# A macaron block on one core: the third pass's matmuls split once more in groups of four tiles, and x added by accumulating transfers

## The chip, the core and the metric

The kernel runs on one core of a Trainium2 chip. The metric is device microseconds of one execution. A core has five engines, each with an instruction queue of its own: TensorE (PE, with weight loads shown apart as PEld), VectorE (DVE), ScalarE (ACT), GpSimd (POOL) and SyncE (SP). DMA transfers are issued from the queues of SP, ACT and POOL. An issue that has to wait holds up everything behind it in its queue.

## The reference

4 x 1024 tokens of 1024 channels go through a feed-forward layer, an attention layer and the same feed-forward layer again, in float32:

```python
dots = softmax(x @ centroids.T / 0.1)              # 64 clusters
hits = dots > 0.01
query_sel, cluster_sel = any(hits, axis=1), any(hits, axis=0)
dense = x @ weight.T + bias
ffn = where(query_sel[:, None] & cluster_sel[assignments][None, :], dense, 0)

x = x + 0.5 * ffn(layernorm(x))
x = x + attention(layernorm(x))
x = x + 0.5 * ffn(layernorm(x))
```

Which output columns of the feed-forward layer count (`cluster_sel`) is known only when all tokens have been through the gate. The attention mixes heads within one token.

## The kernel before, in words

**Tiles and passes.** The 4096 tokens are 32 tiles of 128 (`NT` = 32). A tile is one row buffer of 128 partitions x 1024 float32, 512 KB; all such buffers come from one pool of 26 (`row`, L147, `ROWS`). Pass 1 is the first feed-forward layer (dense product and gate), pass 2 the attention, with the gate and the last 256 columns of the second feed-forward layer (L1347 to the end of the loop), and pass 3 the other 768 columns of that layer, then the mask, the addition of x and the store of the output. Between passes tiles lie in device memory: `y2` holds x after the attention, `xTd` the normalised transposed tile, `d2` the dense product's last 256 columns. Of the tiles 26 to 31 (`KEPT` = 6) x, the transposed tile and the product stay in row buffers from pass 2 to pass 3; they are not stored to `y2`, `xTd`, `d2`.

**Seven block products.** The 768 columns are computed for two tiles at a time with Winograd's form of Strassen's algorithm (`winograd`, L315): tokens x channels and channels x columns are split 2 x 2, and seven block products instead of eight are made, each four matmuls of 128 x 128 by 384 columns (`HALF`). `token_sums` (L293) makes sums s1 to s4 of the tokens on POOL, and `weight_sums` made sums t1 to t4 of the weights in the space of `wqkv`. Results of several products add up in the same PSUM bank (`onto=`), and DVE adds each partial result to the tile's row (L328) and to the bias.

**The inner split of pass 1.** For tiles 4 to 27, pass 1 already works in groups of four tiles (`Group`, L649). Products 1, 5 and 6 are made whole, two tiles each (`outer`, L688). Products 2, 3, 4 and 7, of two tiles x 512 channels x 384 columns, are split once more in the same way: seven inner products, each two matmuls by 192 columns (`inner_product`, L796). It needs sums of the tokens' quarters (`inner_sums`, L636: four POOL operations of 256 columns) and 16 quarter sums of the weights (`inner`). The order of work inside a group is written out by hand: `inner_product` runs its own matmuls and reads and calls `fills` (matmuls of another product) and `works` (DVE work of other tiles) at fixed places. Every engine's queue has exactly the order of the code.

**Pass 3** (L1484 to L1575). For each pair of tiles SP loads the transposed tile, x from `y2`, and the 256 columns from `d2` (`load_3`, L1493), two pairs ahead. POOL adds the bias to the 256 columns and makes the token sums of the next pair (`ahead_3`, L1501). PE runs the seven products. DVE reads the banks, multiplies the row by the row mask and column mask (`masked`, L456), adds x (L1513), and ACT issues the store (`stored`, L1508). The pair 30/31 comes first, because its inputs are in row buffers, then 0/1 to 24/25; the masks and adds of the kept tiles are spread over the first pairs. In the last pair, products 7 and 4 are made in halves of 192 columns, and `finish` (L1545) masks, adds and stores each half straight from the bank.

In pass 2 POOL has, among others, the key expansion (L1196), the attention's scaling and addition of x (L1283, L1287), the store of `y2` (L1359) and of `d2` and `xTd` (L1304, L1305), and at the end the weight sums for pass 3 (L290) and the token sums of the first pairs.

Of the kernel before, what the change touches and what calls it, by code (L numbers as in the profile page):

```python
# [15 lines left out]
P = 128  # L16
# [26 lines left out]
def kernel(  # L43
# [270 lines left out]

    def winograd(a, b, ss, ts, pool, name, held=False, finish=None):  # L315

# [10 lines left out]
        def add(out, ps, other):  # L327
            nc.vector.tensor_tensor(out, ps, other, ALU.add)  # L328
# [31 lines left out]
        yield  # L360
        if finish:
            m = HALF // 2
            ys = [(prod(f"7{i}", s3, t3[:, :, sl]), sl) for i, sl in enumerate((slice(m), slice(m, HALF)))]
            for y, sl in ys:
                add(cb[:, 1, sl], y, ca[:, 1, sl])
        else:
            y = prod(7, s3, t3)
            add(cb[:, 1], y, ca[:, 1])
        if held:
# [14 lines left out]
        yield  # L384
        if finish:
            for y, sl in ys:
                finish(prod(4, a22, t4[:, :, sl], onto=y), sl)
        else:
            prod(4, a22, t4, onto=y)
            add(cb[:, 0], y, cb[:, 0])  # L390
        del xT[a], xT[b]
# [84 lines left out]
    with (  # L476
# [144 lines left out]

        M = HALF // 2
        inner = wqkv.rearrange("p k c -> p (k c)").rearrange("p (s k c) -> p s k c", s=16, k=2)

# [3 lines left out]

        def inner_weights():

            for i, y in enumerate((w21, ts[3], ts[2], w22)):
                yield from weight_sums(
                    quarters(y), [inner[:, 4 * i + j] for j in range(4)], [nc.gpsimd] * 4
                )
# [14 lines left out]
        class Group:  # L649
# [6 lines left out]
            def upper_sums(self):  # L656
                a, b = self.t[:2]
                self.i[2] = inner_sums(xT[a][:, 4:], xT[b][:, 4:], f"2_{a}")

            def sums_0(self):  # L660
# [134 lines left out]

            def inner_product(self, n, fills, works):  # L796

# [12 lines left out]
                s = self.i.pop(n)  # L810
                r1 = 1 + o % 2
                dst = (a, b) if n in (2, 3) else (c, d)

                def mul(j, src, wt, onto=None):
                    ps = onto
                    if onto is None:
                        ps = psum1.tile([P, 512], F32, tag="st", bufs=4, name=f"in{n}{j}_{a}")[:, :M]
                    for k in range(2):
                        nc.tensor.matmul(  # L819
                            ps,  # L820
                            src[:, k, :],
                            wt[:, k, :],
                            start=(k == 0 and onto is None),
                            stop=(k == 1),
                            skip_group_check=onto is not None,
                        )
                    return ps
# [12 lines left out]
                read(0, 0, u)  # L840
                works[0]()
                v = mul(7, s[:, 2], u3)
                fills[0]()
                read(1, 1, v)
                mul(6, s[:, 1], u2, onto=u)
                read(1, 0, u)
                works[1]()
                fills[1]()
                mul(4, hi[:, 2:], u4, onto=v)
                read(1, 0, v)  # L850
                del v
                mul(5, s[:, 0], u1, onto=u)
                read(1, 1, u)
                z = mul(2, lo[:, 2:], y21)
                works[2]()
                read(0, 0, z)
                del z
                fills[2]()
                mul(3, s[:, 3], y22, onto=u)
                read(0, 1, u)  # L860
                works[3]()
# [240 lines left out]
    with (  # L1102
# [192 lines left out]
        def has(t):  # L1295
            return 0 <= t < NT
# [29 lines left out]
        for s in range(NT + 5):  # L1326
# [29 lines left out]
            if s == NT:  # L1356
                next(sums)
            if g >= 0 and g < FIRST_KEPT:
                nc.gpsimd.dma_start(out=y2[g], in_=xt[g])  # L1359
# [128 lines left out]

    with (
        tc.tile_pool(name="psum3", bufs=1, space=bass.MemoryType.PSUM) as psum3,  # L1490
    ):

        def load_3(t):  # L1493
            if t not in xT:
                load_xT(t)
            load_x(t, y2[t], 3)
            dt_[t] = row(f"d4_{t}")
            lo = PARTS[2][0]
            nc.sync.dma_start(out=dt_[t][:, lo:], in_=d2[t][:, lo:])

        def ahead_3(a):  # L1501

            for t in (a, a + 1):
                tail = dt_[t][:, PARTS[2][0] :]
                nc.gpsimd.tensor_tensor(tail, tail, brow[:, PARTS[2][0] : EMB], ALU.add)
            return token_sums(xT, a, a + 1, 2)

# [3 lines left out]
        def added(t, sl=slice(0, EMB), store=True):  # L1511
            masked(dt_[t], t, 1, mask, sl)
            nc.vector.tensor_tensor(xt[t][:, sl], xt[t][:, sl], dt_[t][:, sl], ALU.add)  # L1513
            if store:
                stored(t, sl)

        gates_used()
        for t in range(2):
            load_3(t)
        t = NT - 2  # L1520
# [6 lines left out]
        mask = row_mask(clusters, hot, 1)  # L1527
        ss = ahead_3(0)
        kept = iter(range(FIRST_KEPT, NT))
        next(steps)  # L1530
        added(next(kept))
        next(steps)
        added(next(kept))
        for _ in range(2):
            next(steps)
        for t in range(2, 4):
            load_3(t)
        done = iter(())
        for a in range(0, FIRST_KEPT, 2):
            last = a + 2 == FIRST_KEPT  # L1540
            for t in (a + 4, a + 5):
                if t < FIRST_KEPT:
                    load_3(t)

            def finish(ps, sl):  # L1545
                t = FIRST_KEPT - 1
                d = dt_[t][:, sl]
                nc.vector.scalar_tensor_tensor(
                    d, ps, qsel[1][:, t : t + 1], mask[:, sl], ALU.mult, ALU.mult
                )  # L1550
                nc.vector.tensor_tensor(xt[t][:, sl], xt[t][:, sl], d, ALU.add)
                stored(t, sl)

            steps = winograd(a, a + 1, ss, ts, psum3, 3, finish=finish if last else None)
            if not last:
                ss = ahead_3(a + 2)
            tail = slice(2 * HALF, EMB)
            part = slice(0, HALF), slice(HALF, 2 * HALF)
            for i in range(7):
                next(steps)  # L1560
                for t in done if i in (0, 1 if last else 2) else kept if i in (4, 5) else ():
                    added(t)
                    break
                if a + 4 == FIRST_KEPT and i in (4, 5):
                    added(a + i - 2, tail)
                if last:

                    for t, sl in {
                        2: ((a, part[0]),),
                        3: ((a + 1, part[0]),),  # L1570
                        4: ((a + 1, part[1]),),
                        5: ((a, part[1]),),
                    }.get(i, ()):
                        added(t, sl, store=i != 3)
            done = iter((a, a + 1))  # L1575

# [42 lines left out]
```

## Time and profile before

| | us |
|---|---|
| median of three runs | 1290.11 (1288.87 to 1292.22) |
| the profiled execution | 1289.28 |
| its span, from the first to the last instruction | 1287.5 |
| PE, DVE, ACT, POOL busy | 1270.3, 927.9, 469.0, 724.2 |
| granted TensorE clock | 1.00 |
| pass 3: first products of pair 30/31 at, last matmuls from | 1028.4, 1280.9 |

In a line of the profile, `out<-in` are the program's names of the tiles an instruction writes and reads, `xN` is a count, and the brackets at the end give idle time before it and what ended that. Matmuls overlap, so the duration of one is longer than the distance between two; the pace is read from the starts. A float32 matmul of the code shows as two MATMUL records.

### The profile page before, as it was taken

How to read it: one execution, taken by the hardware profiler on the slowest of the kernel's cores; microseconds unless marked ns; L12 is line 12 of the kernel's file. 1: busy time of each engine (PE TensorE's matmuls, PEld its weight loads, DVE VectorE, ACT ScalarE, POOL GpSimd, SP SyncE). 2: the span in 40 equal slices, each digit the busy share in tenths (PEclk: the TensorE clock that was granted, in tenths of full speed). 3: DMA queues.
4: the chain of work that ended last, by engine and by line, in shares of the span. 5: the costliest groups of instructions: out<-in, count | busy, mean ns of one | idle time of the engine just before them, and what ended most of it. 6: DMA issues, size and time to landing. Idle time of an engine off the chain costs nothing.

```text
span 1287.5 us, 23368 instructions
## 1 busy us (share of the span) xinstructions
PE 1270.3 (99%) x8970; PEld 872.5 (68%) x8970; DVE 927.9 (72%) x1862; ACT 469.0 (36%) x736; POOL 724.2 (56%) x624
## 2 busy tenths in 40 slices
PE   8999999999999999999999999999999999999998
PEld 7578898898885666666666666666665655555555
DVE  5657777777777368888888888888876348555546
ACT  4312222222301356766666676666632300000000
POOL 2981533533534457666787877776747416633440
PEclk9999999999999999999999999999999999999999
DMA  9553545554555357677677777777561257565422
GB/s 308 110 164 84 147 117 122 173 162 135 169 192 195 92 161 230 182 202 219 220 225 223 223 217 237 224 221 236 157 188 31 102 163 255 202 213 192 174 107 82
DMA packets 191127, 227.12 MB, mean 176 GB/s; under 512 B 118184, under 2 KB 146728, under 8 KB 191016
## 3 DMA queue, kind: packets, MB, share of 16 engines
q1 hardware_dynamic: 170892, 171.33, 45.0%
q0 software_dynamic: 11232, 37.49, 8.4%
q10 hardware_dynamic: 8892, 16.81, 3.7%
q8 instruction: 71, 1.16, 0.4%
q14 instruction: 40, 0.33, 0.1%
HBM read 134.59 MB, written 90.99 MB: 175 GB/s over the span
## 4 chain that ended last, share of the span: by engine, by line
PE 84%; DVE 8%; DMA 3%; ACT 2%; POOL 2%; issue 1%; SPq 0%; DVEq 0%; ACTq 0%; POOLq 0%
PE st L337 27%; PE qs L1140 14%; PE ff L263 10%; PE in L819 8%; PE la L736 7%; PE st L700 7%; PE pq L263 3%; PE tp L230 3%; PE po L1258 2%; PE sc L1216 2%; DVE d L458 1%; DMA qkvd<-qkv 1%; POOL wqkv L290 1%; DVE bn L170 1%; DVE o L1270 1%
## 5 line engine op out<-in xcount | busy, mean ns | idle before, releaser
L263 PE MATMUL ff<-wc,xT 128*128 128x320 f32 x640 | 179.3, 433 | 2.2 <-DVE d L328 1.2
L263 PEld LDWEIGHTS ff<-wc,xT 128*128 128x128 f32 x640 | 119.9, 190 | 51.5 <-ACT xT L231 1.5
L337 PE MATMUL st<-wqkv,ts 128*128 128x384 f32 (+1 forms) x392 | 129.6, 480 | 2.1 <-POOL wqkv L290 2.1
L328 DVE TENSOR_TENSOR d<-st,d 128x384 f32<-128x384 f32 (+1 forms) x102 | 55.9, 551 | 96.3 <-PE st L337 95.5
L500 ACT ACTIVATE xb<-xb,scb 128x256 f32<-128x256 f32 x108 | 56.0, 590 | 162.0 <-DVE d L837 67.9
L1140 PE MATMUL qs<-wc,ts_2q 128*128 128x384 f32 x336 | 114.4, 490 | 0.0
L337 PE MATMUL st<-wc,xT 128*128 128x384 f32 x320 | 110.0, 487 | 0.0
L337 PEld LDWEIGHTS st<-wqkv,ts 128*128 128x128 f32 x392 | 73.9, 190 | 52.5 <-POOL wqkv L290 2.3
L469 POOL TENSOR_TENSOR x<-x,d 128x1024 f32<-128x1024 f32 x32 | 75.4, 2358 | 55.0 <-DVE d L458 40.1
L302 POOL TENSOR_TENSOR ts<-xT 128x512 f32<-128x512 f32 x20 | 25.7, 1285 | 140.9 <-PE st L337 74.7
L1196 POOL TENSOR_TENSOR kd<-qk,tmask 128x1024 f32<-128x1024 f32 x32 | 60.6, 1894 | 77.4 <-DMA qk<-qkvd 77.4
L458 DVE SCALAR_TENSOR_TENSOR d<-d,qsel,mask 128x1024 f32<-128x1024 f32 (+2 forms) x68 | 95.0, 1397 | 0.2
L1140 PEld LDWEIGHTS qs<-wc,ts_2q 128*128 128x128 f32 x336 | 62.6, 190 | 43.7 <-issue 3.2
L337 PEld LDWEIGHTS st<-wc,xT 128*128 128x128 f32 x320 | 60.4, 190 | 41.5 <-issue 0.6
L1287 POOL TENSOR_TENSOR x<-x,ot 128x1024 f32<-128x1024 f32 x32 | 78.2, 2445 | 2.5
L1140 PE MATMUL qs<-wqkv,xT 128*128 128x384 f32 x224 | 78.3, 492 | 0.0
L231 ACT COPY xT<-tp 128x512 f32<-128x512 f32 x112 | 59.4, 581 | 46.9 <-PE tp L230 46.9
L665 POOL TENSOR_TENSOR os<-xT 128x512 f32<-128x512 f32 x12 | 15.2, 1270 | 101.0 <-DVE sc L179 101.0
L837 DVE TENSOR_TENSOR d<-in,d 128x192 f32<-128x192 f32 (+1 forms) x168 | 64.9, 398 | 9.0 <-PE in L819 5.1
L700 PE MATMUL st<-ws,os 128*128 128x384 f32 x192 | 65.8, 486 | 0.0
L230 PEld LDWEIGHTS tp<-ident,xn 128*128 128x128 f32 x448 | 56.9, 191 | 12.9 <-issue 2.0
L220 ACT ACTIVATE xn<-x,sc 128x1024 f32<-128x1024 f32 x30 | 49.9, 1664 | 37.3 <-DVE sc L215 37.3
(197 smaller groups left out, 2764.4 us busy)
## 6 DMA issues: line engine op xcount, KB each, us to landing
x<-in_L_attn_x_dram SPq DMA_DIRECT2D x64, 512.0 KB
d<-d SPq DMA_DIRECT2D x64, 512.0 KB
out_dram<-x ACTq DMA_DIRECT2D x30, 512.0 KB
xb<-in_L_attn_x_dram SPq DMA_DIRECT2D x108, 128.0 KB
y<-x POOLq DMA_DIRECT2D x26, 512.0 KB, 3.8
xTd<-xT POOLq DMA_DIRECT2D x26, 512.0 KB, 6.0
xT<-xTd SPq DMA_DIRECT2D x26, 512.0 KB
x<-y SPq DMA_DIRECT2D x26, 512.0 KB
```

Source lines behind the costliest of these rows:

```text
L230: nc.tensor.transpose(tp[:, j, :], channels(xn)[:, k], ident)
L263: nc.tensor.matmul(p, src[:, k, :], wts[:, k, lo:hi], start=(k == 0), stop=(k == KT - 1))
L337: nc.tensor.matmul(ps, src[:, k, :], wts[:, k, :], start=(k == 0 and onto is None), stop=(k == 3), skip_group_check=onto is not None,)
L458: nc.vector.scalar_tensor_tensor(d[:, sl], d[:, sl], qsel[which][:, t : t + 1], mask[:, sl], ALU.mult, ALU.mult)
L469: nc.gpsimd.tensor_tensor(xt[t], xt[t], dt_.pop(t), ALU.add)
L700: nc.tensor.matmul(ps, src[:, k, :], wt[:, k, :], start=(k == 0 and n == 1), stop=(k == 3), skip_group_check=n != 1,)
L736: nc.tensor.matmul(ps[:, i], src[:, k, :], wt[:, k, :], start=(k == 0 and i == 0 and first is not None), stop=(k == 3), skip_group_check=i ...
L819: nc.tensor.matmul(ps, src[:, k, :], wt[:, k, :], start=(k == 0 and onto is None), stop=(k == 1), skip_group_check=onto is not None,)
L837: nc.vector.tensor_tensor(v, ps, v, ALU.add)
L1140: nc.tensor.matmul(ps, src[:, k, :], wts[:, k, :], start=(k == 0 and onto is None), stop=(k == 3), skip_group_check=onto is not None,)
L1196: nc.gpsimd.tensor_tensor(kd, qk[:, :, D:].unsqueeze(2).to_broadcast([P, NBLK, 4, D]), tmask.unsqueeze(1).unsqueeze(3).to_broadcast([P, NB ...
L1287: nc.gpsimd.tensor_tensor(xv, xv, ov, ALU.add)
```

## The change

Pass 3 takes pass 1's scheme for tiles 0 to 23, in six groups of four; the pair 24/25 goes ahead of them and stays as it was.

- Inner products: `inner_product` is turned into a generator, `parts`, and pass 3 runs two of them side by side (`both`): products 2 and 4, then 7 and 3. Between the inner products stand the outer ones (5 of this group, 1 and 6 of the next) and DVE's work: masks of the group before, s1 and s2 of the next group (512 columns each, DVE in place of POOL), the bias of the 256 columns (DVE in place of POOL).
- The 16 quarter sums of the weights are made again, by DVE, in a tile of their own.
- x is no longer loaded for these tiles. After the mask, a transfer from POOL's queue reads `y2` and adds it to the row in place (`accum_op=ALU.add`), and the store follows it. This also holds for the pair 24/25 and the kept tiles, whose x is now stored to `y2` in pass 2 (six more stores). Tiles 20 and 21 of the last group load x and add it on DVE and, for one part, on POOL.
- The last pair's halves and `finish` go; in the last group products 2 and 3 are interleaved by hand, and the last inner product is masked and added straight from the bank.

```diff
-    def winograd(a, b, ss, ts, pool, name, held=False, finish=None):
+    def winograd(a, b, ss, ts, pool, name, held=False):
...
-            if g >= 0 and g < FIRST_KEPT:
+            if has(g):
                 nc.gpsimd.dma_start(out=y2[g], in_=xt[g])
...
+            def sums_12(self, engine, which=(0, 1)):
...
+                for i in which:
+                    lo, hi = self.t[i], self.t[i + 2]
+                    engine.tensor_tensor(s1[:, i], xT[hi][:, :4], xT[hi][:, 4:], ALU.add)
+                    engine.tensor_tensor(s2[:, i], s1[:, i], xT[lo][:, :4], ALU.subtract)
...
+        def summed(t):
+            xt[t] = dt_[t]
+            nc.gpsimd.dma_start(out=xt[t], in_=y2[t], accum_op=ALU.add)
+            stored(t, slice(0, EMB))
+
+        def finished(t):
+            masked(dt_[t], t, 1, mask)
+            summed(t)
...
+        def both(x, y, fills, works):
+            for p in (x, y):
+                next(p)
+            works[0]()
+            fills[0]()
+            for p in (x, y, x, y):
+                next(p)
+            works[1]()
+            fills[1]()
+            for p in (x, y):
+                next(p)
+            works[2]()
+            for p in (x, y, x, y):
+                next(p)
+            works[3]()
+            for p in (x, y):
+                next(p)
+            fills[2]()
+            for p in (x, y):
+                next(p)
+            works[4]()
...
+            if not last:
+                g.sums_34()
+                for t in nxt.t:
+                    load_tail(t)
+                both(
+                    g.parts(2, w_bank),
+                    g.parts(4, w_bank),
+                    (lambda: g.outer(5, 0), lambda: g.outer(5, 1), lambda: nxt.outer(1, 0)),
+                    (
+                        one_masked(0),
+                        one_masked(1),
+                        then(one_masked(2), summing(0, 1)),
+                        one_masked(3),
+                        then(summing(2, 3), lambda: nxt.sums_12(nc.vector, (0,))),
+                    ),
                 )
...
+                nxt.lower_sums()
...
+                    nxt.upper_sums()
+                    nxt.sums_3(False)
+                both(
+                    g.parts(7, w_bank),
+                    g.parts(3, w_bank),
+                    (lambda: nxt.outer(1, 1), lambda: nxt.outer(6, 0), lambda: nxt.outer(6, 1)),
+                    (
+                        lambda: nxt.sums_12(nc.vector, (1,)),
+                        lambda: tail_biased(nxt.t[2]),
+                        lambda: tail_biased(nxt.t[3]),
+                        then(lambda: tail_biased(nxt.t[0]), lambda: early_tail(0)),
+                        then(lambda: tail_biased(nxt.t[1]), lambda: early_tail(1)),
+                    ),
+                )
+            else:
+                a, b, c, d = g.t
+                g.outer(5, 0)
+                g.outer(5, 1)
+                g.upper_sums()
+                g.sums_4()
+                both(
+                    g.parts(7, w_bank),
+                    g.parts(4, w_bank),
+                    (nothing,) * 3,
+                    (
+                        one_masked(0),
+                        one_masked(1),
+                        then(one_masked(2), summing(0, 1)),
+                        one_masked(3),
+                        summing(2, 3),
+                    ),
+                )
...
+                x, y = g.parts(2, w_bank), g.parts(3, w_bank)
+                first, second = slice(0, HALF), slice(HALF, 2 * HALF)
+                next(x)
+                next(x)
+                masked(dt_[d], d, 1, mask)
+                summed(d)
+                next(y)
+                next(x)
+                masked(dt_[c], c, 1, mask)
+                summed(c)
...
+                added(b, second)
+                next(y)
+                added(a, second, store=False)
+                y.send(last_part)
```

A generator of `parts` makes, in order: inner product 1; 7; 6 (onto the bank of 1); 4 (onto the bank of 7); 5 (onto the bank of 1); 2 (a bank of the other pool); the read of 2; 3 (onto the bank of 1). `one_masked(j)` masks a tile of the group before, or in the first group finishes the pair and makes quarter sums; `summing` issues the accumulating transfers and the stores; `sums_34` makes s3 and s4 and the inner sums of products 7 and 3 on POOL, `lower_sums` and `upper_sums` those of products 4 and 2.

## The prediction

> **What bounds the kernel now.** I read the engine table first, then the chain of waits, then the order of time on TensorE (PE).
>
> ```profile
> PE 1270.3 (99%) x8970; PEld 872.5 (68%) x8970; DVE 927.9 (72%) x1862; ACT 469.0 (36%) x736; POOL 724.2 (56%) x624
> ```
>
> PE is busy 99% of the span. The chain, asked from 950 us on, ends so:
>
> ```profile
> 1038.35 245.35 PE st L337 x776
> 1283.70 0.03 issue
> 1283.72 0.43 DVE d L1548
> 1284.15 0.02 issue
> 1284.17 0.36 DVE x L1551
> ```
>
> From 1038 us the third pass is one unbroken run of matmuls, then 0.8 us of VectorE (DVE), and 1287.50 - 1284.53 = 2.97 us of store and end. So PE time saved there is span saved, unless another engine or a transfer becomes late. How fast small matmuls go is read in the first pass, where groups of four tiles already use the inner split. PE in order of time (start, duration of the merged row; the next row's start tells the pace):
>
> ```profile
> 102.37 0.81 PE L819 MATMUL in<-wqkv,is 128*128 128x192 f32 x4
> 103.02 0.81 PE L819 MATMUL in<-ws,xT 128*128 128x192 f32 x4
> 103.67 2.74 PE L700 MATMUL st<-ws,os 128*128 128x384 f32 x8
> 106.25 0.81 PE L819 MATMUL in<-ws,is 128*128 128x192 f32 x4
> ```
>
> Four records of 192 columns take 0.65 us (102.37 to 103.02), eight of 384 take 2.58 us (103.67 to 106.25). (The code's two matmuls show as four records, its four as eight.) Half the columns thus cost 0.504 of the time: the split loses almost nothing here. The row means in the groups' view (326 and 486 ns) would say 0.67 and turn the change into a loss; they are latencies of overlapping matmuls and must not be used.
>
> The Trainium skill, page "TensorE: Matmul & The Clock Gate", section "Back-to-back issue gap", speaks against small matmuls: with weight loads between, a sustained stream is paced by both, and it gives 81 ns at 128 columns where streaming alone would be 56 ns. If 192 columns cost 45% over their share, a four-record chunk would take some 0.94 us (an estimate from that page) and the change would lose about 5 us a group; the rows above show that this does not happen at this shape.
>
> **The change, part by part.**
>
> *Matmuls.* Per four tiles the old code runs two pairs of seven products, 14 x 2.58 = 36.12 us (the steps at 1061.60, 1064.18, 1066.76 us are 2.58 apart throughout). The new code keeps products 1, 5, 6 (two tiles each, 6 x 2.58 = 15.48) and makes the other four by seven inner products of 0.65 each: 4 x 7 x 0.65 = 18.20. Together 33.68, so 2.44 us less; six groups: **-14.6 us**. Tiles 24 and 25 stay a pair and only move ahead.
>
> *Six more y2 stores on POOL.* A POOL store of y takes 0.60 us (its 26 issues: 15.5 us) and waits about 0.30 us for the add before it (7.7 us over 26). Late in the second pass POOL is once on PE's path:
>
> ```profile
> 954.31 1.89 POOL L1196 TENSOR_TENSOR kd<-qk,tmask 128x1024 f32<-128x1024 f32 x1 [16.37 <-DMA qk<-qkvd]
> ```
> ```profile
> 978.65 2.85 PE L337 MATMUL st<-wqkv,ts 128*128 128x384 f32 x8 [2.12 <-POOL wqkv L290]
> ```
>
> Stores of tiles 26 and 27 vanish in the 16.4 us of idle; that of 28 falls after it and before the weight sum that PE awaits; those of 29 to 31 come behind it. **+0.9 us**.
>
> *DVE inside the groups.* A group needs 21 reads of 192 columns, 7 of 384, 8 outer reads, four masks, four sums s1/s2 of 512 columns, and four tail biases. Rows: 0.348, 0.548, 0.555, 1.385 (third pass, 1050 to 1230 us), 0.425 for 256 columns; 512 lie between 0.557 (384) and 1.545 (1024), about 0.72. Sum 7.3 + 3.8 + 4.4 + 5.5 + 2.9 + 1.7 = 25.7 us beside 33.7 of PE. It is uneven: the half with products 2 and 4 holds all masks, about 15.5 us in 16.84; the other half holds 10. Laid out chunk by chunk, the tightest chain in the full half is the fifth inner product's result, read at 13.7 us, against PE's third product onto the same bank at 15.5: 1.9 us of slack. So 0. The old adds of x (1.5 us a tile) are what makes room.
>
> *Inner weight sums, and the start.* Sixteen DVE subtractions of 384 columns, 16 x 0.557 = 8.9 us. Eight lie beside pair 24/25 (DVE there: 5.0 of reads, 5.5 of masks, 4.5, 1.7 of biases, in 18.06 us), eight in group 0, where only two masks are due. Each set is finished at least 3 us before its product. POOL's sums for group 0 (16 of 256 columns at 0.73, 8 of 512 at 1.27, 22 us) have from about 1045 to 1094 us. 0.
>
> *Accumulating transfers.* No row shows one. PE does not wait for them directly, but the built program's waits show two row buffers that they hold up: POOL's sums for the next product 7 reuse the row of the previous group's last tile, and DVE's first s1 of the next group reuses the row of the first one; both must first be masked, summed and stored. Call T the time from issue to stored row. In a group's own time: last mask at 14.8, issue at 15.4, row free at 15.4 + T; then POOL makes 8 sums of 256 and 2 of 512 (8.4 us) before it can issue the next group's first transfer, whose row is free at 24.4 + 2T. DVE can come to that s1 as late as 19.6 us into the next group without PE noticing. So a group takes max(33.7, 4.8 + 2T): free up to T = 14.4. The nearest rows for T: POOL's plain stores of the same 512 KB, 2.9 to 5.0 us to land (y), median 6.0 (xTd), and the wait for an output store by SyncE:
>
> ```profile
> DMA to landing us min/median/max: 2.9/3.8/5.0
> ```
> ```profile
> SPq L1499 <- DMA out_dram<-x: 43.3, 16, 4.5
> ```
>
> Low end: 3.8 + 4.5 = 8.3. High end: twice 6.0 plus the longest output wait, 5.8, = 17.8. I take 6 + 4.6 = 10.6, nearest to the row of the same queue. DMA share in the third pass was 0.55 at 190 GB/s, so there is room. Hence 0 in the groups; at the high end four waiting groups pay 6.7 us each, +27.
>
> The Trainium skill, page "Collectives: The Full Stack", section "The bandwidth ceiling: the fold count and why AG ≠ RS ≠ AR", says that an add in the transfer needs two source reads and so runs at about half the pace of a copy. No run here shows it yet; by that rule the moving part doubles, and an estimate of T from it would be about 11 to 13, still under the limit.
>
> *The end.* The old end was arranged so that DVE had 0.8 us left. In the new one the last group has no outer products of a next group between its inner ones: PE needs 5.16 + 28 x 0.65 = 23.4 us, and DVE in the same stretch 2.2 (outer reads) + 3.8 + 20 x 0.348 + 6 masks x 1.276 + 3 x (0.618 + 0.557) + 0.62 + 0.77 = 25.6 us. Its first reads cannot start before 2.8 us and it idles until 6.4 for product 7; from there 23.4 us are left, so it ends at 29.8, or about 27 if independent operations overlap by 0.08 us as these do:
>
> ```profile
> 1278.72 0.61 DVE L328 TENSOR_TENSOR d<-st,d 128x192 f32<-128x192 f32 x2
> ```
>
> (two of 0.349). I take 28.3, against 24.4 if DVE kept up. Beside it the mask of tile 22 ends at about 21: transfer, ACT issue 0.34 and store 4.6 end at 32.5; the last rows, 28.3 + 3.3 (twice the old last store), at 31.6. Against 24.4 + 2.97 = 27.4 this is **+5.2 us** (bounds +2.7 and, with T at its high end, +12).
>
> **Sum**, against the profiled execution of 1289.28 us (span 1287.5, 1.8 around it): 1289.28 - 14.6 + 0.9 + 5.2 = 1280.8. The median of the runs shown, 1290.11, is 0.8 above that execution, so I say **1281 us**.
>
> **Rivals.**
>
> *Transfers set the pace (slower).* If T passes 14.4 us, DVE stands before s1 at the end of each first half, all later reads with it, and PE on its banks. From T = 15.5 the four groups give back the 8.5 us; at 16.5 (transfer 12, store 4.6) +16.5: **1297**. For: the DMA slices at 1050 to 1122 us reach 0.73, and nothing here shows an accumulating transfer. Against: the rows of 3.8 to 6.0.
>
> *DVE becomes the bound in the full half.* POOL will be busy about 57% of a group (19 of 33.7 us; 40% before), and DVE's two-input operations stretch beside POOL:
>
> ```profile
> 1093.23 2.17 DVE L458 SCALAR_TENSOR_TENSOR d<-d,qsel,mask 128x1024 f32<-128x1024 f32 x1
> ...
> 1111.30 1.27 DVE L458 SCALAR_TENSOR_TENSOR d<-d,qsel,mask 128x1024 f32<-128x1024 f32 x1
> ```
>
> Three masks at 2.17 in place of 1.27 use up 2.7 us, 0.8 more than the slack: five groups, about +4.5, **1285.5**, and more if the s1 sums stretch too.
>
> *The end costs nothing* (overlaps are larger, the transfer of tile 22 is short): **1276**.
>
> **Chances.** Forecast (1278 to 1285) 0.62, transfers 0.13, DVE 0.16, short end 0.09. About 0.3% is what a measurement of this kernel can tell from no change, 3.9 us: faster ends at 1286.2. Faster: 0.62 + 0.09 + a little under half of the DVE case 0.06 = 0.77; same 0.09; slower 0.14. The range 1276 to 1292 takes in the short end and DVE, and leaves out most of the transfer case.
>
> **What will show it.** The inner matmuls of the third pass 0.65 us apart per chunk, each steady group 33.7 us long, and PE's idle time small until the last group. PE waiting for DVE there and 3 to 6 us of DVE after the last matmul would show the end as costed. A wait of DVE's s1 sums for an output store, at the middle of groups 1 to 4, would show the transfer rival; masks above 2 us with PE waiting for reads, the DVE rival. POOL's wait at 978 us should grow by under 1 us. I am wrong if groups take over 35 us, or the end is bound by something else, such as the last output stores.

## The result, and the profile after

| | before | after |
|---|---|---|
| median, us (range) | 1290.11 (1287.54 to 1292.76, 7 runs) | 1305.47 (1298.64 to 1309.85, 7 runs) |
| ratio, 95% interval | | 1.0106 (1.0074 to 1.0139) |
| profiled execution / its span, us | 1289.28 / 1287.5 | 1305.47 / 1303.7 |
| first product of pair 30/31 at | 1028.42 | 1028.91 |
| pass 3, from there to the end of the span | 259.1 | 274.8 |

The change made the kernel 1.1% slower, where I had forecast 0.7% faster. The seven executions of after fall into three of 1298.64 to 1299.38 us and four of 1305.47 to 1309.85; the profiled one, whose account follows, is of the slower four, and no trace shows where the others gained. By the prediction's terms pass 3 should have taken 259.1 - 14.6 + 5.2 = 249.7 us; it took 274.8. So 25.1 us have to be found.

The engine table of after, first:

```profile
PE 1265.5 (97%) x9242; PEld 911.2 (70%) x9242; DVE 964.7 (74%) x2010; ACT 469.1 (36%) x736; POOL 775.2 (59%) x711
```

PE is busy for 4.8 us less and the span is 16.2 us longer: PE now waits. The pace itself came out as costed. PE in order of time at the start of group 1 (start, duration of the merged row):

```profile
1117.55 0.81 PE L851 MATMUL in<-wc,xT 128*128 128x192 f32 x4
1118.20 0.81 PE L851 MATMUL in<-wqkv,xT 128*128 128x192 f32 x4
1118.85 2.74 PE L733 MATMUL st<-wqkv,os 128*128 128x384 f32 x8
1121.43 2.76 PE L851 MATMUL in<-inner,is 128*128 128x192 f32 x16
```

0.65 us per inner chunk, 2.58 per outer one; the groups that start at 1083.87, 1117.55 and 1192.82 us take 33.68 us each, the predicted number to the hundredth (groups are counted from 0; group 1 begins at 1117.55). All rows of PE in pass 3 before which it waited, ahead of the last group:

```profile
1076.94 7.09 PE L733 MATMUL st<-wqkv,os 128*128 128x384 f32 x16 [4.31 <-DVE d L743]
1178.46 2.93 PE L851 MATMUL in<-inner,is 128*128 128x192 f32 x8 [5.05 <-DVE d L869]
1250.69 1.68 PE L851 MATMUL in<-inner,is 128*128 128x192 f32 x8 [2.00 <-DVE d L869]
```

All three name DVE. With them the account closes:

| place | predicted, us | measured, us | difference |
|---|---|---|---|
| four outer chunks before group 0 | 10.32 | 16.57 | 6.25 |
| group 2 | 33.68 | 41.59 | 7.91 |
| group 4 | 33.68 | 37.64 | 3.96 |
| last group, from its first chunk to the end | 32.5 | 39.56 | 7.06 |
| sum | | | 25.2 |

**Before group 0** DVE is late by its own work. DVE in order of time, four of its rows, and one row of POOL:

```profile
1054.83 0.55 DVE L290 TENSOR_TENSOR inner<-wc 128x384 f32<-128x384 f32 x1
...
1065.13 4.19 DVE L290 TENSOR_TENSOR inner<-wqkv,inner 128x384 f32<-128x384 f32 x1
...
1070.25 1.08 DVE L290 TENSOR_TENSOR inner<-wqkv,inner 128x384 f32<-128x384 f32 x1
...
1071.72 4.14 DVE L1560 TENSOR_TENSOR d<-d,brow 128x256 f32<-128x256 f32 x4
```
```profile
1065.79 3.11 POOL L673 TENSOR_TENSOR os<-xT,xT 128x512 f32<-128x512 f32 x2
```

A weight sum takes 0.55 us while POOL issues a transfer and 1.08 or more beside POOL's sums; one of them takes 4.19 us and spans two whole sums of POOL. The four biases take 4.14 us, though one alone takes 0.41. Meanwhile DVE's reads of banks (L328, L743) stay at 0.54 to 0.56 us. POOL's own order of time tells why its sums fall just there:

```profile
1044.77 0.92 POOL L1573 DMA_DIRECT2D d<-y  x1 [13.30 <-DVE d L448]
```

POOL stood 13.3 us before the first accumulating transfer, whose mask was not made yet, and all its sums for group 0 stood behind it.

**In group 2** DVE and POOL both wait for an output store. In the names, `os` is a row of the sums s1 to s4, `is` a row of the inner sums, `d` a tile's result and `out_dram` the output, so that `DMA out_dram<-d` is a store. Who waited for what from 1150 to 1196 us (total, times, longest), and POOL in order of time:

```profile
POOL os L673 <- DMA out_dram<-d: 8.3, 1, 8.3
DVE os L665 <- DMA out_dram<-d: 7.9, 1, 7.9
```
```profile
1131.68 0.86 POOL L1573 DMA_DIRECT2D d<-y  x1 [0.86 <-DVE d L869]
...
1149.71 0.73 POOL L634 TENSOR_TENSOR is<-os 128x256 f32<-128x256 f32 x1 [0.97 <-DMA out_dram<-d]
...
1160.14 1.77 POOL L1573 DMA_DIRECT2D d<-y  x2
```

DVE's s1 waits until 1176.5 for the row of a transfer issued at 1160.14: T = 16.4 us. In group 4 it is 14.8 (1233.93 to 1248.74). ACT could issue the first store at 1166.38, so transfer and store took about 6 and 10 us; in group 4 they took 5.4 and 9.4. Within a group the later transfers land later: the four of group 2 take from 6.2 to 14.9 us, with a median of 10.4.

The stall of group 2 begins in group 1. The last transfer there is issued at 1131.68, and POOL's inner sum that reuses its row starts only at 1149.71: T = 18.0. POOL comes out of the sums behind it at 1160.14, 8.9 us into group 2. After the stall POOL has caught up: it issues the first transfer 3.9, 8.9, 3.4 and 7.4 us into groups 1 to 4, and groups 2 and 4 are those that stall.

**At the end** DVE's last operation ends at 1293.40, 29.3 us after the group's start (predicted 28.3), and the span 10.3 us later. ACT's queue, merged by form:

```profile
1278.56 19.02 ACTq L1563 DMA_DIRECT2D out_dram<-d  x6
1297.68 2.28 ACTq L1563 DMA_DIRECT2D out_dram<-x  x4
```

The four stores of tiles 20 and 21 stand behind the six whole rows, each of which waits for its accumulating transfer. The last of these is issued at 1285.14 and takes 12.0 us to land, so its store could be issued only at 1297.2, the stores behind it later still, and the span ends at 1303.7.

### The profile page after: what moved, and what is told of

It is laid out like the page before. It is cut to its first block, busy times and chain, and to the rows that moved or that the text cites. A ratio compares the mean times of both kernels' runs of the same rounds, so it can differ in the third digit from the quotient of the medians.

```text
span 1303.7 us, 24127 instructions
## 1 busy us (share of the span) xinstructions
PE 1265.5 (97%) x9242; PEld 911.2 (70%) x9242; DVE 964.7 (74%) x2010; ACT 469.1 (36%) x736; POOL 775.2 (59%) x711
## 4 chain that ended last, share of the span: by engine, by line
PE 80%; DVE 9%; DMA 5%; POOL 2%; issue 2%; ACT 1%; SPq 1%; DVEq 0%; ACTq 0%; POOLq 0%
PE qs L1192 17%; PE in L851 14%; PE st L733 13%; PE ff L263 10%; PE st L337 8%; PE la L769 7%; PE pq L263 3%; PE tp L230 3%; PE sc L1268 2%; PE po L1310 2%; DVE d L448 2%; DMA d<-y 1%; DMA x<-in_L_attn_x_dram 1%; DVE d L869 1%; POOL wqkv L290 1%
## 5 line engine op out<-in xcount | busy, mean ns | idle before, releaser
L869 DVE TENSOR_TENSOR d<-in,d 128x192 f32<-128x192 f32 (+1 forms) x335 | 127.6, 400 | 17.8 <-PE in L851 11.0
L743 DVE TENSOR_TENSOR d<-st,brow 128x384 f32<-128x384 f32 x96 | 51.1, 554 | 77.4 <-PE st L733 75.5
L733 PE MATMUL st<-wqkv,os 128*128 128x384 f32 x192 | 70.2, 513 | 4.3 <-DVE d L743 4.3
L851 PE MATMUL in<-wqkv,is 128*128 128x192 f32 x336 | 68.5, 327 | 1.3 <-DVE d L869 1.2
L733 PE MATMUL st<-wc,xT 128*128 128x384 f32 x192 | 65.5, 486 | 0.0
L1573 POOL DMA_DIRECT2D d<-y x30 | 26.1, 888 | 65.8 <-DVE d L448 50.8
L220 ACT ACTIVATE xn<-x,sc 128x1024 f32<-128x1024 f32 x30 | 49.9, 1664 | 33.7 <-DVE sc L215 33.7
L851 PEld LDWEIGHTS in<-wqkv,is 128*128 128x128 f32 x336 | 56.9, 190 | 6.7 <-DVE d L869 1.5
```

What stands on the lines that cost most here:

```text
L733: nc.tensor.matmul(ps, src[:, k, :], wt[:, k, :], start=(k == 0 and n == 1), stop=(k == 3), skip_group_check=n != 1,)
L851: nc.tensor.matmul(ps, src[:, k, :], wt[:, k, :], start=(k == 0 and onto is None), stop=(k == 1), skip_group_check=onto is not None,)
L869: nc.vector.tensor_tensor(v, ps, v, ALU.add)
```

## The experiments

My theory after this reading: the accumulating transfer is slow, and beside the loads and stores of a group it fills the DMA engines (T about 16 in place of 10.6), which costs 11.9 us in groups 2 and 4 and 7 at the end; and the start is DVE stretched by POOL. Rivals: the second transfer per tile hurts whatever it does; the groups stall by DVE's and POOL's own load; the start stalls by transfers. The passes before the third, alike in the kernels with the change, took 1027.7 to 1034.7 us from one execution to another; so I compare **pass 3 of each profiled execution** besides the times. Each ratio is to the kernel before as it ran beside that kernel, with medians of 1288.35 to 1290.94 us.

| kernel | median, us | ratio to before, 95% | pass 3, us | four chunks before group 0 | groups 0 to 4 over 33.68 | end after DVE's last |
|---|---|---|---|---|---|---|
| before | 1290.11 | | 259.1 | | | |
| after | 1305.47 | 1.0106 (1.0074 to 1.0139) | 274.8 | 16.57 | 7.9 + 4.0 | 10.3 |
| without x | 1285.57 | 0.9961 (0.9946 to 0.9976) | 249.7 | 10.55 | 0 | 3.2 |
| plain copy | 1290.68 | 0.9996 (0.9979 to 1.0013) | 255.6 | 13.94 | 0 | 5.7 |
| one transfer | 1287.42 | 0.9977 (0.9960 to 0.9994) | 255.6 | 16.55 | 0 | 3.1 |
| accumulating alone | 1290.05 | 1.0002 (0.9982 to 1.0022) | 259.1 | | | |
| one row more | 1313.28 | 1.0205 (1.0186 to 1.0223) | 282.1 | 16.45 | 10.3 + 0.7 + 8.2 | 10.4 |
| weight sums on POOL | 1300.18 | 1.0063 (1.0035 to 1.0091) | 273.7 | 11.26 | 9.2 + 7.6 | 9.7 |
| biases later (one transfer) | 1286.03 | 0.9971 (0.9955 to 0.9987) | 253.1 | 10.79 | 3.0 | 3.2 |
| POOL's order (one transfer) | 1283.95 | 0.9950 (0.9935 to 0.9965) | 251.3 | 12.21 | 0 | 3.1 |
| one transfer, lighter start | 1283.62 | 0.9961 (0.9945 to 0.9977) | 249.4 | 10.32 | 0 | 3.1 |

### Without x

```diff
             xt[t] = dt_[t]
-            nc.gpsimd.dma_start(out=xt[t], in_=y2[t], accum_op=ALU.add)
             stored(t, slice(0, EMB))
```

> Leaves out the addition of x for tiles 0 to 19 and 22 to 31: the accumulating transfer is gone, the masked row is stored at once; everything else stays. Theory T (the two stalls inside the groups, 7.9 us in group 2 and 4.0 in group 4, and most of the 10.3 us between DVE's last operation and the end come from the accumulating transfers, through row buffers that they hold and through ACT's queue, whose stores wait for them): all groups take 33.7 us, the end follows DVE's last operation by about 3.5 us, and the start stall of 6.3 us stays: 1305.5 - 11.9 - 6.8 = about 1287 us. Rival D (the group stalls are DVE's and POOL's own load, two-input operations stretched beside each other): only the end shortens, about 1298.5 us, and PE still waits some 12 us inside the groups.

Measured: 1285.57. The groups run at 33.68, the end is short: the transfers cause both, DVE's and POOL's load does not. One thing I had not expected: the start stall went too (16.57 to 10.55), without a change to DVE's work. POOL then makes the first half of group 0's sums (s1, s2 and the inner sums of products 4 and 2) from 1036 to 1047 us, before DVE's first weight sum at 1059.6.

### A plain copy in place of the accumulation

```diff
-            nc.gpsimd.dma_start(out=xt[t], in_=y2[t], accum_op=ALU.add)
+            nc.gpsimd.dma_start(out=xt[t], in_=y2[t])
```

> Plain copies in the place of the accumulating transfers: the same bytes of y2 go to the same rows from the same queue, so the rows of tiles 0 to 19 and 22 to 31 hold x alone and the layer's part is left out there. Theory A (it is the accumulation that is slow: 8.3 us to land against 3.7 for a plain store of 512 KB): T falls from about 16 to about 10, under the 14.4 us that are free, the groups take 33.7 us and the end is some 4 us shorter: about 1289 to 1290 us. Rival B (a second transfer of 512 KB per tile in itself fills the DMA engines, whatever it does): copies land in 7 us or more, and at least half of the 12 us of group stalls stays: 1297 us or more.

Measured: 1290.68, no stall in the groups. Theory A holds: the number of transfers and their bytes are those of after, and only the addition is gone. The DMA view from 1029 to 1300 us (packets, MB, share of 16 engines; then us to landing), of after:

```profile
q0 software_dynamic: 4320, 15.73, 31.2%
...
d<-y POOLq DMA_DIRECT2D x30, 512.0 KB, 8.3
```

and of this kernel:

```profile
q0 software_dynamic: 4320, 15.73, 17.6%
...
d<-y POOLq DMA_DIRECT2D x30, 512.0 KB, 5.3
```

The packets of the same 15.73 MB take 31.2 / 17.6 = 1.77 times as long on the DMA engines. The quickest transfer landed in 5.3 us against 3.7; one issue took POOL 0.87 us against 0.54.

### One transfer in place of two

```diff
-                nc.gpsimd.dma_start(out=y2[g], in_=xt[g])
+                nc.gpsimd.dma_start(out=rows(of, g) if direct(g) else y2[g], in_=xt[g])
...
             xt[t] = dt_[t]
-            nc.gpsimd.dma_start(out=xt[t], in_=y2[t], accum_op=ALU.add)
-            stored(t, slice(0, EMB))
+            nc.gpsimd.dma_start(out=rows(of, t), in_=xt[t], accum_op=ALU.add)
```

`direct(t)` is true for all tiles but 20 and 21.

> One transfer in place of two: pass 2 stores x of tiles 0 to 19 and 22 to 31 straight into the output, and pass 3 adds the masked row to the output by one accumulating transfer from POOL's queue; ACT has no store for these tiles. Theory T (a row is held by accumulating transfer and store in turn, about 16 us): it is held by one transfer of 8 to 10 us, all groups take 33.7 us, the end is bound by DVE's last operation plus a store or by the last accumulating transfer, and the start stall stays: about 1287 us. Rival M (accumulating into device memory is slower than into the row, 15 us or more each, or the six at the end queue up): groups keep half of their stalls or the end stays at 10 us: 1295 us or more.

Measured: 1287.42, against the expected 1287. A row is now held by one transfer, and the addition happens in device memory. Issues of this kernel in the same window:

```profile
out_dram<-d POOLq DMA_DIRECT2D x30, 512.0 KB, 6.0
```

6.0 us (10.6 at most) hold the row in place of about 16; all groups take 33.68, the end follows DVE's last operation by 3.1 us. Only the start stall is left (16.55).

### The accumulation alone, in the old pairs

The kernel before, without loads of x and additions for tiles 0 to 23:

```diff
-            nc.vector.tensor_tensor(xt[t][:, sl], xt[t][:, sl], dt_[t][:, sl], ALU.add)
+            if t < FIRST_KEPT - 2:
+                xt[t] = dt_[t]
+                nc.gpsimd.dma_start(out=xt[t], in_=y2[t], accum_op=ALU.add)
+            else:
+                nc.vector.tensor_tensor(xt[t][:, sl], xt[t][:, sl], dt_[t][:, sl], ALU.add)
```

> The kernel before with one half of the change alone: its pairs and seven block products stay, and for tiles 0 to 23 the loading of x and DVE's addition are replaced by the accumulating transfer into the row and the store behind it (the kept tiles and the last pair keep DVE's addition). Theory F (the transfer only hurts where a group of four makes four at once and hands its rows on at once): two transfers per 18 us and the rows that x no longer takes leave enough slack, PE stays unbroken, 1289 to 1291 us. Rival Q (an accumulating transfer costs by itself: POOL's queue waits for masks, stores wait for transfers, rows come late for any schedule): PE waits in the pairs, 1295 us or more.

Measured: 1290.05, pass 3 259.1 as before. Its page and its DMA view:

```profile
PE 1270.9 (99%) x8970; PEld 873.1 (68%) x8970; DVE 892.4 (69%) x1838; ACT 468.8 (36%) x736; POOL 731.0 (57%) x648
```
```profile
d<-y POOLq DMA_DIRECT2D x24, 512.0 KB, 6.5
```

DVE has 35 us less to do and nothing comes of it, for PE is the bound. Two transfers per 18.06 us land in 6.5 us and hold nobody up. The groups differ from this in two things: four transfers come within a few microseconds, beside four loads, and their rows are handed on at once. No run separates the two.

### One row more

```diff
+        s1_own = sums3.tile([P, EMB], F32, name="s1_own")
...
-                    self.s[1], self.s[2] = outer_sum(f"1_{a}"), outer_sum(f"2_{a}")
+                    self.s[1] = s1_own.rearrange("p (t k c) -> p t k c", t=2, k=4)
+                    self.s[2] = outer_sum(f"2_{a}")
```

> The change as it is, with both transfers, and one row buffer more: s1 of every group has a buffer of its own, so that a group takes 15 rows from the pool of 26 in place of 16, and a row comes round after 26/15 groups (58.4 us) in place of 26/16 (54.7 us). Theory T (what DVE and POOL wait for in groups 2 and 4 is rows that transfer and store still hold): each of the two stalls (7.9 and 4.0 us of the groups' time) shrinks by about 3.6 us or goes, 4 to 7 us less: 1298 to 1301 us by the profiled execution of 1305.5; start stall and end stay. Rival X (the DMA engines are full there and something else than a row is late, a load or a copy that PE needs): the groups stay at 41.6 and 37.6 us, 1304 to 1306 us.

Measured: 1313.28, worse by 8 us, and group 2 takes 10.3 us too long; both expectations missed. Who waited from 1150 to 1200 us:

```profile
POOL is L634 <- DMA out_dram<-d: 17.1, 1, 17.1
DVE os L667 <- DMA out_dram<-d: 10.4, 1, 10.4
```

My arithmetic took the pool for a ring. The built program shows another hand-out: s2 now gets the row that s1 had, that of the first tile transferred, and the row that a load of a transposed tile used to wait for goes to an inner sum of product 4. In after, SP's four loads were spread over 15 to 19 us by these waits in groups 1 to 3; here they go out in 4 us, on top of the four accumulating transfers, whose median landing grows to 9.4 us. So the rows do carry the stall, but a row more moved the wait from a load, which has time, to sums, which have none.

### The start: weight sums on POOL

```diff
-        wsums = inner_weights(nc.vector)
+        wsums = inner_weights()
...
         ss = token_sums(xT, *pair, 2)
+        for _ in wsums:
+            pass
```

The two places before group 0 and the two in it where DVE made four of them each are gone.

> The sixteen quarter sums of the weights are made by POOL in one go before it issues the first accumulating transfer (it idles 13.3 us there), and no longer by DVE beside pair 24/25 and in group 0. Theory S (the 6.3 us of PE's stall before group 0 are DVE's: eight weight sums of 384 columns and four biases stretched by POOL's work beside them): the wait of outer product 6 for DVE, 4.3 us, and the slow pace after it vanish, four outer products take 10.3 us in place of 16.6, and the time falls by about 6 us to 1299 us. Rival R (the stall comes from the transfers or from POOL's sums for group 0 being late): PE waits there as before, 1304 to 1306 us, or more, since POOL is put back by up to 3 us.

Measured: 1300.18, 5.3 us less than after. The intervals of the two ratios overlap, so it is the profile that shows the gain: the wait fell from 4.31 to 0.70 us. The profiled execution is the slowest of ten (1291.94 to 1307.05): its groups 2 and 4 lost 9.2 and 7.6 us, so the gain shows in the start alone. The biases still suffer. DVE in order of time, here with POOL's sums beside all four:

```profile
1068.05 6.85 DVE L1560 TENSOR_TENSOR d<-d,brow 128x256 f32<-128x256 f32 x4
```

### The start: biases later

On the kernel with one transfer, the four biases of group 0 move from ahead of its outer products to its two empty mask places, behind the weight sums there.

```diff
-        for t in g.t:
-            tail_biased(t)
...
                         for _ in range(4):
                             next(wsums)
+                        for t in g.t[2 * j - 4 : 2 * j - 2]:
+                            tail_biased(t)
```

> The kernel with one accumulating transfer straight into the output, with the weight sums on DVE as in the change, and only the four biases of group 0's tiles moved from before group 0 into it. Theory B (the four biases, 4.1 us in DVE's queue between the last read of pair 24/25 and the first outer read, are what PE waits for): the wait of 4.3 us goes and the slow matmuls after it, 1281 to 1283 us. Rival W (the weight sums, stretched from 0.56 to 1.1 to 1.4 us each, are the larger part, and more of DVE's work follows in group 0): the wait shrinks by less than 2.5 us, 1285 us or more.

Measured: 1286.03, in the range of rival W, though the wait went as theory B had it. PE's waits (lines are 3 higher here than in after):

```profile
1074.35 5.40 PE L736 MATMUL st<-wqkv,os 128*128 128x384 f32 x16 [0.23 <-DVE d L746]
1101.28 1.57 PE L854 MATMUL in<-inner,is 128*128 128x192 f32 x8 [0.82 <-DVE d L872]
1104.52 1.57 PE L854 MATMUL in<-inner,is 128*128 128x192 f32 x8 [1.67 <-DVE d L872]
```

The biases were what PE waited for; but group 0 has no room for weight sums and biases together and gives 3.0 us of it back, as rival W had it.

### The start: POOL's order alone

On the kernel with one transfer, POOL's first sums of group 0 (and SP's loads for them) move ahead of the first accumulating transfer:

```diff
         ss = token_sums(xT, *pair, 2)
+        groups = [Group(a) for a in range(0, BY_GROUP, 4)]
+        g = groups[0]
+        for t in g.t:
+            load_xT(t)
+        g.sums_12(nc.gpsimd)
+        g.lower_sums()
+        g.upper_sums()
```

> The kernel with one accumulating transfer straight into the output, and only POOL's order before group 0 changed: its sums s1, s2 and the inner sums of products 2 and 4 of group 0 (and the loads that they need) come before the first accumulating transfer in place of after it. DVE's work is as in the change. Theory O (POOL sits 13 us before that transfer, whose mask is not made yet, and so its sums fall on DVE's weight sums and biases and stretch them): the start stall goes as it went in the kernel without x, and the pass from the first product of pair 30/31 to the end takes 250 us in place of 255.6, the time is 1281 to 1283 us. Rival L (DVE's own load makes the stall, where POOL's sums stand does not matter): PE waits 4 us before outer product 6 as before, 1286 us or more.

Measured: 1283.95; pass 3 251.3, 4.3 us less. Theory O holds for two thirds of the stall: a wait of 1.65 us is left, where s3, s4 and the inner sums of group 0 (1066.36 to 1078.9) still lie beside DVE's last weight sums and the biases. DVE's first weight sums, in order of time, are back at their own length:

```profile
1057.81 0.55 DVE L293 TENSOR_TENSOR inner<-wc 128x384 f32<-128x384 f32 x1
1058.40 0.56 DVE L293 TENSOR_TENSOR inner<-wc,inner 128x384 f32<-128x384 f32 x1
```

### One transfer and a lighter start

One transfer, weight sums on POOL, and biases inside group 0.

> The kernel with one accumulating transfer straight into the output, and beside it a lighter start: POOL makes the sixteen weight sums before its first transfer, and DVE adds the biases of group 0's four tiles inside group 0 in place of before it. Theory S (the start stall is DVE's queue, stretched by POOL; nothing else is left): four outer products before group 0 take 10.3 us, the groups 33.7 us each, and the time is 1287.4 - 6.3 = about 1281 us, 0.7% under the kernel before. Rival P (16 us more of POOL ahead of group 0's sums make POOL late there): PE waits for sums of group 0, 1284 us or more.

Measured: 1283.62 (1279.80 to 1288.09). PE in order of time into group 0:

```profile
1073.05 5.32 PE L736 MATMUL st<-wc,xT 128*128 128x384 f32 x16
1078.21 5.32 PE L736 MATMUL st<-wqkv,os 128*128 128x384 f32 x16
1083.37 0.81 PE L854 MATMUL in<-wc,xT 128*128 128x192 f32 x4
```

10.32 us, no wait; pass 3 takes 249.4 us against the 249.7 that the prediction gives for it. The time expected, 1281, lies within the runs but under their median: the profiled execution came to pass 3 only at 1034.71 us, 5.8 later than after did. This kernel and the one with POOL's order changed beat both before and after; between the two the intervals decide nothing.

## Why the prediction was wrong, by its own steps

- **Matmuls, -14.6: right.** 33.68 us in every group that waited for nothing, in all kernels. (The loss that the prediction gives for chunks of 0.94 us comes to 28 x 0.94 + 15.48 - 36.12 = 5.7 us a group, not about 5; nothing rests on it.)
- **y2 stores, +0.9: not shown.** Pass 3 began 0.5 us later, but that start varies by 6 us between executions. PE's wait for POOL was 2.18 us (2.12 before), hardly longer; the eight records after it took 4.25 us in place of 2.85 at a granted clock of 0.50 (978.94 to 982.35 us), of which more below.
- **DVE inside the groups, 0: right.** With the transfers out of the way DVE's full half fits: in group 1 DVE was busy for 25.7 of 33.68 us, as summed.
- **Weight sums and the start, 0: wrong, 6.25 us.** The step priced sixteen sums at 0.557 and four biases at 0.425 us beside 22 us of POOL's sums that the same paragraph put there, and priced the stretch only as a rival inside the groups. It also counted POOL's sums as starting at about 1045 us without seeing that the first accumulating transfer, waiting for a mask, is what holds them until then. Moving POOL's sums ahead of it took 4.3 us away, and with fewer operations on DVE all 6.2.
- **Accumulating transfers, T = 10.6, so 0 in the groups: the step that failed, by size.** The mechanism was the one named: s1 and POOL's sums wait for rows that transfer and store still hold, free up to T = 14.4. T was 18.0 for the last transfer of group 1 and 16.4 for the first of group 2. Put into the prediction's own chain, 24.4 + 18.0 + 16.4 - 33.7 = 25.1 us after group 2's start for the row of s1, where 19.6 are free; measured were 25.3. Chosen was 6 + 4.6. For the first transfer of a group the 6 was right (6.2 and 5.4 in groups 2 and 4), for the later ones not (up to 14.9), and the store behind the first took 10.0 and 9.4. The 4.6 came from SyncE's waits for a store in a pass at half load, and such a wait need not be the store's whole time. Here the accumulation takes 1.77 times the engine time of a copy, and from 1160 to 1182 us, with four transfers, four loads and four stores, the share of the DMA engines was 0.96. The rival "transfers set the pace" is what happened, at 11.9 us over the groups where it gave 16.5 for T = 16.5: only every other group stalled, and 2.7 and 1.8 of the 11.9 us are PE's slow clock after its waits, which the prediction did not have.
- **The end, +5.2: its DVE part was right (29.3 against 28.3), its transfer part not.** Tile 22's transfer and store were put at 32.5 us after the group's start with the same T; the transfer alone landed at 33.0 (1297.2), and the end came at 39.56, near the upper bound that the prediction gives for a T at its high end. With one transfer per tile the end came 32.3 us after the group's start. That this is close to 32.5 is luck: it is DVE's last operation and a store that end there.

The Trainium skill's page "Collectives: The Full Stack", section "The bandwidth ceiling: the fold count and why AG ≠ RS ≠ AR", says of the add of a ReduceScatter that it needs two source reads and runs at half the pace of a copy; the page says it of a ring of cores, and the 1.77 of this case is near it. The prediction had weighed that rule and put T at 11 to 13 by it; it left out that the later transfers of a group and the stores behind them take longer too.

## What to carry to other kernels

Price a new kind of transfer by the engine time that it takes from everything beside it, not by its own landing: ask what else moves in the same few microseconds, and which sum or load gets the row that it holds. An issue that waits holds all work behind it in its queue (13.3 us of POOL here), and what is pushed back may then collide with another engine's work; so look where the pushed work lands. When a data movement happens twice (into the row, then out), see whether the addition can be made on the way out.

## What the runs showed of the hardware that I had not expected

- **Accumulating transfers** of 512 KB: 31.2% of the DMA engines' time from 1029 to 1300 us against 17.6% for plain copies of the same bytes; landing 8.3 against 5.3 us median over pass 3, 6.5 in pairs, 6.0 into device memory without a store behind.
- **DVE beside POOL.** Operations of DVE with both operands in SBUF tiles took 0.55 us alone and 1.08 to 4.19 beside POOL's sums before group 0 (384 columns), and four biases of 256 columns 4.14 and 6.85 us in place of 4 x 0.41; those that read a PSUM bank stayed at 0.54 to 0.56. The Trainium skill, page "SBUF — State Buffer", section "Who interferes with whom", says the same: a DVE instruction with two SBUF inputs contends with a GpSimd instruction that reads SBUF, one with at most one, outside the page's 2-port modes, does not.
- **A wait of PE can cost more than its length.** After the wait of 5.05 us, 8 records of 192 columns took 2.72 us to the next row in place of 1.30, and 8 of 384 took 3.86 in place of 2.58: 2.7 of group 2's 7.9 us. After 4.31 us, 16 records took 6.93 in place of 5.16, and after 2.00 us the two rows took 5.67 in place of 3.88. After 3.38 us (plain copy) and 1.65 (POOL's order) the pace was whole at once. The granted clock shows why. In after it is 0.50 from 1077.93 to 1081.34, from 1176.91 to 1183.74 and from 1252.01 to 1255.42 us, that is for 3.41 us or twice that, and these starts lie 98.98 and 75.10 us apart, 29 and 22 times 3.413. So time is laid out in stretches of 3.41 us, and what counts is how long PE is idle within one. Two stretches of after around the wait of 2.00 us, then the two of the plain copy that share its 3.38 us (busy time of PE, PEld, DVE, ACT and POOL, then the clock, the DMA share and GB/s):

```profile
1248.60:1252.01 3.41, 1.41 (x9) 1.33 (x9) 3.20 (x6) 0.00 (x0) 0.00 (x0) 1.00 1.06 274
1252.01:1255.42 3.41, 3.41 (x8) 1.90 (x7) 2.63 (x7) 0.00 (x0) 2.33 (x2) 0.50 0.85 321
```
```profile
1075.23:1078.64 3.41, 1.49 (x5) 0.57 (x3) 3.41 (x4) 0.00 (x0) 3.41 (x3) 1.00 0.75 275
1078.64:1082.06 3.42, 1.96 (x6) 1.25 (x7) 1.78 (x4) 0.00 (x0) 2.99 (x5) 1.00 0.13 41
```

In after PE idles 2.00 us within one stretch, and the next is at half clock; the longer wait of the plain copy is parted into 1.92 and 1.46 us, and the clock stays whole. The same parts before from after ahead of pass 3: of 2.12 us of wait 1.89 fall into one stretch of before (976.76 to 980.17, counted back by 3.41 us from 1287.37, where its clock falls after the last matmul), and the clock stays at 1.00; of 2.18 us 2.12 fall into one of after (975.53 to 978.94), and the next is at 0.50. The most that left the clock whole in these traces after their first 60 us is 1.92 us, the least that halved it 1.94 (one transfer, 975.77 to 979.18).
- **The spread.** Passes 1 and 2 varied by some 6 us between executions of the same code there; why stays open. A difference of a few microseconds in pass 3 is better read in its own stretch.
